# A conv and attention block whose order of work is planned ahead: product and hidden buffers handed out by the plan, other planning numbers, another table of places

## Chip, cores and metric

The kernel runs on one core of one Trainium2 chip. The metric is the device time of one execution in microseconds. The kernel before took 4097.11 us, the median of 3 runs (4096.09 to 4097.49).

## What is computed

The reference is one transformer block on x of 16 images, 128 channels, 96 x 96 pixels, in float32:

```python
xn1 = layernorm(x)                      # over the 128 channels of a pixel
q, k, v = xn1 @ wq.T, xn1 @ wk.T, xn1 @ wv.T
a = softmax(l2norm(q) @ l2norm(k).T * 0.25)   # 8 heads, 16 x 16 over channels
x = x + (a @ v) @ wp.T
h1 = conv1x1(layernorm(x), w_in)        # 128 -> 512 channels
h3 = gelu(depthwise_conv3x3(h1, w_dw))
out = x + conv1x1(h3, w_out)            # 512 -> 128
```

## The kernel before, in words

Channels lie on the 128 partitions. An image is 8 bands of 12 rows; band g runs over all 16 images (128 bands). The 512 hidden channels are 4 chunks of 128. A **conv job** (g, n) is the depthwise convolution of chunk n of band g, 12 x 96 = 1152 elements a partition. There are 470 jobs with accumulating DMAs and one last job without. In some bands chunk 3 is done by matmuls instead (`by_matmuls`, L1037, gelu L1047).

One conv job goes through all engines. TensorE makes h1 (L928) into one of four PSUM banks; ScalarE copies it to the job's `h1` tile (L933, and two halo rows by L924). Of the nine taps, ScalarE makes three as products (L944, tiles `pr`), GpSimd adds the first product and the centre tap into `merged` (L947), and VectorE does the remaining five: the **first tap** (L956, `acc<-h,ratio,merged`, the only tap with two inputs in SBUF), three taps on the PSUM accumulator (L960), and the **last tap**, which writes the tile `h3` (L956, `h<-h,ratio,acc`). The other two products come in by DMA: the **first add** (L969, `pr<-pr`) adds the third product to the second, and the **second add** (L972, `h<-pr`) adds that sum to `h3`. Both are issued by GpSimd. ScalarE then does the gelu (L976) in place in `h3`, four matmuls a third of a band (L1065) give the output, VectorE adds it to x (L1072) and SyncE stores it (L1076).

Beside the jobs runs the normalization of the next image (names with `a`) and of the next band (`b`), 288 groups of 512 pixels each: transposes (L654, L658), a copy by ScalarE to a tile `zT` (L690), statistics on VectorE (L665), variance, power and scaling on GpSimd (L670, L674, L696), and transposes back on TensorE (L741), which ScalarE places in `xn` (L745, L747). The attention matmuls with the image's mixing matrix (L606) give x after attention, by ScalarE (L615), to which an accumulating DMA adds x (L618, GpSimd). SyncE loads x (L586).

The order of all this is written by a planner at build time (class `Plan`, L76 on). Each piece of work is recorded by `op` with its engine, an estimated duration, what it reads and writes, and a place: the job's number plus an offset out of the table `AT` (a few kinds have a `RANK` too). `order` then plays the pieces through: whenever an engine is idle it takes the ready piece with the lowest place. A piece is ready when those it needs have ended by plan, `SLACK` included. For an accumulating DMA the end is one serial line: `max(issue + WAIT, line) + T_ADD`, plus a margin. The planner also hands out buffers (`free`, `slot`): a piece that needs a new buffer waits until one is free by plan, and gets the one that was freed longest ago. The pieces are emitted in the order of their planned starts; on the chip each engine works through its own instructions in that order and waits for semaphores.

In the kernel before, the tiles `pr` (7 buffers) and `h3` (8) came from rotating pools (`prp`, `h3p`): the planner's numbers for them paced the plan, but which buffer a tile really got was decided by the pool.

`two` marks pieces that share a lock in the planner: first taps on VectorE, and the merge L947 and the scaling L696 on GpSimd. A marked GpSimd piece waits for a running first tap, and a first tap waits for a running marked GpSimd piece.

Of the kernel before, what the change touches and what calls it, by code (L numbers as in the profile page):

```python
# [18 lines left out]
BR = 12  # L19
# [17 lines left out]
QT = 4  # L37
# [9 lines left out]
ZT_BUFS = 7  # L47
IN_TURN = ("zT", "tr", "h3", "pr", "xb", "x1")
AT = dict(
    load_w=8.85, weights=-1115.55, zeros=-3007.1, load_a=9.15, forth_a=-13.45, stats_a=342.05, variance_a=451.45,  # L50
    power_a=3765.3, pool_product=152.05, merge=371.35, scaled_a=3441.05, gram=419.9, back_a=415.35, place_a=450.55,
    attention=4.2, mix=1645.7, residual=204, mixed=450.15, add_x=3459.55, forth_b=-8.15, stats_b=-221.5,
    variance_b=332.25, power_b=311.5, shift_b=20.9, scaled_b=245.4, back_b=-36.7, place_b=740.05, halo=1030.45,
    hidden=418.25, kept=-261.05, products=719.4, add_last=374.1, tap=4.75, add_first=-2841.6, gelu=934.15,
    conv=420.9, conv_gelu=4.6, out=422.4, add=-1132.95, store=144.25, mix_0=441.5, residual_0=6.4, mixed_0=991.85,
    add_x_0=3457.3, gram_0=-32.2, forth_a_0=1643.1, forth_b_0=-7.6, stats_a_0=-369.9, stats_b_0=511.45,
    scaled_a_0=-2763, copied_a=-1171.4, copied_b=-1171.6, copied_a_0=4, copied_b_0=906.8, scaled_b_0=451.9,
    back_a_0=-31.55, back_b_0=260.7, place_a_0=995.05, place_b_0=577.35, shift_b_0=22.8, late=-369.55,
)
RANK = dict(tap=-1415.25, products=337.1, forth_a=-1411.95, forth_b=-1558.5, conv_gelu=-1485.55, mix=-1412.45)  # L60
STEP = dict(scaled=0.3, hidden=0.1, products=0.5, tap=0.166, conv=1.6, conv_tap=0.03, out=0.8, out_part=0.05)
SLACK = 300
NORM1_END = 6.0
EARLY = 5
WAIT = dict(POOL=350, SP=1300, ACT=1300)
T_START = 2300
T_VARIANCE = 420
T_POWER = 350 + 165 * QT * QB
T_SMALL = 220
T_MERGE = 2400  # L70
T_POOL_PRODUCT = 1190
T_SCALED = 225
T_ADD, T_MOVE = 3060, 1640


class Place(float):  # L76
# [8 lines left out]
class Plan:  # L85
# [44 lines left out]
    def order(self):  # L130
        ops, free = self.ops, self.free
        left = [len(o[4]) for o in ops]
        followers = [[] for _ in ops]
        for k, o in enumerate(ops):
            for d in o[4]:
                followers[d].append(k)
        held = [[] for _ in ops]
        pending = {}
        for t, ks in self.users.items():
            pending[t] = len(ks)  # L140
            for k in ks:
                held[k].append(t)
        queues, idle, waiting = {}, {}, {}
        queue_of = {p: [] for p in free}
        for k, o in enumerate(ops):
            queues.setdefault(o[0], [])
            idle[o[0]] = True
            for t in o[5]:
                queue_of[t[0]].append((getattr(o[2], "turn", o[2]), k))
        turn = {p: sorted(q)[::-1] for p, q in queue_of.items()}  # L150
        events, starts, count = [], [None] * len(ops), 0

        def push(time, kind, what):
            nonlocal count
            count += 1
            heapq.heappush(events, (time, count, kind, what))

        def room(k):
            need = {}
            for t in ops[k][5]:  # L160
                need[t[0]] = need.get(t[0], 0) + 1
                if t[0] in IN_TURN and turn[t[0]][-1][1] != k:
                    return t[0]
            for p, n in need.items():
                if len(free[p]) < n:
                    return p
            return None

        def dispatch(engine, time):
            queue = queues[engine]  # L170
            while queue:
                item = heapq.heappop(queue)
                k = item[1]
                lacks = room(k)
                if lacks is None:
                    break
                waiting.setdefault(lacks, []).append(k)
            else:
                return
            o = ops[k]  # L180
            starts[k] = time
            idle[engine] = False
            for t in o[5]:
                self.slot[t] = free[t[0]].pop(0)
                if t[0] in IN_TURN:
                    turn[t[0]].pop()
                    wake(t[0], time)
            ns, result, own = o[1], o[6], o[7]
            if o[8]:
                self.dma = max(time + ns + WAIT[engine], self.dma) + o[8]  # L190
                result = own = self.dma + result - time
            elif engine == "POOL" and o[9]:
                rest = max(0, self.two - time)
                ns, result, own = rest + ns, rest + result, rest + own
                self.held = time + ns
            if o[9] and engine == "DVE":
                rest = max(0, self.held - time)
                ns, result, own = rest + ns, rest + result, rest + own
                self.two = time + ns
                self.lost += rest  # L200
            push(time + own, "own", k)
            push(time + ns, "idle", k)
            push(time + result, "done", k)

        def wake(pool, time):
            for k in waiting.pop(pool, ()):
                heapq.heappush(queues[ops[k][0]], (ops[k][2], k))
                push(time, "look", ops[k][0])

        for k, o in enumerate(ops):  # L210
            if not left[k]:
                heapq.heappush(queues[o[0]], (o[2], k))
        for e in queues:
            push(0.0, "look", e)
        while events:
            time, _, kind, what = heapq.heappop(events)
            if kind != "look":
                for f in followers[what] if kind != "idle" else ():
                    if (ops[f][0] == ops[what][0]) == (kind == "own"):
                        left[f] -= 1  # L220
                        if not left[f]:
                            heapq.heappush(queues[ops[f][0]], (ops[f][2], f))
                            push(time, "look", ops[f][0])
            if kind == "done":
                for t in held[what]:
                    pending[t] -= 1
                    if not pending[t]:
                        free[t[0]].append(self.slot[t])
                        wake(t[0], time)
            if kind in ("done", "own"):  # L230
                continue
            if kind == "idle":
                what = ops[what][0]
                idle[what] = True
            if idle[what]:
                dispatch(what, time)
        assert None not in starts, "the buffers do not suffice"
        self.end = max(starts)
        return [ops[k][3] for k in sorted(range(len(ops)), key=lambda k: (starts[k], k))]
# [3 lines left out]
def tile_restormer_block(  # L243
# [101 lines left out]
    att = ctx.enter_context(tc.tile_pool(name="att", bufs=1))  # L345
    keep = ctx.enter_context(tc.tile_pool(name="keep", bufs=2))
    h1p = ctx.enter_context(tc.tile_pool(name="h1p", bufs=1))
    prp = ctx.enter_context(tc.tile_pool(name="prp", bufs=PR_BUFS))
    h3p = ctx.enter_context(tc.tile_pool(name="h3p", bufs=H3_BUFS))

# [1 line left out]


    merged = h1p.tile([P, BR, W], F32, name="merged")
    zT_bufs = [h1p.tile([P, QT, P + 1], F32, name=f"zT_{k}") for k in range(ZT_BUFS)]

    def window(t, r, n, dx=0):
# [18 lines left out]

    def z_unit(i, u):
        return ("z", ring_of(i, u * UR) // UR)  # L380

    def rows(t):
        return t.rearrange("p (r w) -> p r w", w=W)
# [42 lines left out]
        op("POOL", ns, p, f, r, w, ns + 80 + SLACK, ns + 80, two=port)  # L426

    def add(p, f, r, w):
        op("POOL", 930, p, f, r, w, 1400 + SLACK, dma=T_ADD)

    def move(p, f, r, w, ns, first=0):
        op("SP", 60 + first, p, f, r, w, 900 + SLACK, dma=ns)
# [16 lines left out]
    def weights(p):  # L449
# [2 lines left out]
        v, names = staged, iter(range(99))  # L452

        def loads():
            a, b = (h3p.tile([P, BR * W], F32, tag="h3", name=f"weights_{k}") for k in range(2))
            v["win"] = a[:, :HID].rearrange("p (n c) -> p n c", c=P)
            v["wout"], v["wp"] = a[:, HID : 2 * HID], a[:, 2 * HID : 2 * HID + P]
            v["wqk"], v["wqkT"] = b[:, : 2 * P], b[:, 2 * P : 4 * P]
# [131 lines left out]
    def norm(i, second, place_of):  # L590
# [41 lines left out]
        def pixels(s, m):  # L632
# [43 lines left out]
            def zT(q):  # L676
# [3 lines left out]
                    zTs[q] = zT_bufs[plan.slot["zT", (name, q)]]  # L680
                    return zTs[q]
                two = [k for k in (q - q % 2, q - q % 2 + 1)]
                t = h3p.tile([P, BR * W], F32, tag="h3", name=f"zT_{two[0]}")
                for k in two:
                    zTs[k] = t[:, k % 2 * QT * (P + 1) : (k % 2 + 1) * QT * (P + 1)].rearrange("p (t c) -> p t c", c=P + 1)
                    nc.gpsimd.memset(zTs[k][:, :, P:], 1.0)
# [93 lines left out]
    def attention(s, i):  # L780
# [27 lines left out]
            nc.scalar.copy(sb([P, P + 1], "gs"), grams[i][:, : P + 1])  # L808
            v["gsb"], v["s"] = v["gs"][:, :P], v["gs"][:, P:]

        @step("PE", 760)
        def _():

            nc.tensor.matmul(ps([P, 2 * P], "ps_u"), lhsT=v["gsb"], rhs=wqkT, start=True, stop=True)
# [18 lines left out]
        def _():  # L833
            nc.vector.tensor_mul(v["prod"], v["ps_u"], wqkT)

        @step("PE", 1100, wide)
        def _():
            pn, pc = ps([P, 2], "ps_n"), ps([P, 2], "ps_c")
            for z in range(2):
# [6 lines left out]
            nc.tensor.matmul(kq, lhsT=v["sk"], rhs=cqk[:, :P], start=False, stop=False)  # L846
            nc.tensor.matmul(kq, lhsT=cqk[:, P:], rhs=v["sqn"], start=False, stop=True)

        @step("DVE", 320)
        def _():  # L850

            n2 = sb([P, 2], "n2")
# [21 lines left out]

            nc.scalar.activation(sb([P, P], "e"), v["ps_qk"], AF.Exp, scale=v["rq"])

        @step("DVE", 700)
        def _():
            em = sb([P, P], "em")
            nc.vector.tensor_mul(em, v["e"], blocks)  # L880
# [22 lines left out]

    def h3_of(g, n):
        if (g, n) not in h3s:
            h3s[g, n] = h3p.tile([P, BR, W], F32, tag="h3", name=f"h3_{g}_{n}")
        return h3s[g, n]

    def conv_job(j, g, n):
# [27 lines left out]
            return window(h1_, dy, BR, dx)  # L937

        def product(t):
            to = d["pr", t] = prp.tile([P, BR, W], F32, tag="pr", name=f"pr_{g}_{n}_{t}")  # L940
            if t == by_pool:
                nc.gpsimd.tensor_scalar(to, shifted(t), ratio[:, n, t : t + 1], 1.0, ALU.mult, ALU.mult)
            else:
# [206 lines left out]
```

## Time and profile before

| what | value |
|---|---|
| runs, median of 3 | 4097.11 us (4096.09 to 4097.49) |
| the profiled execution, its own time | 4102.16 us |
| span of its instructions | 4100.5 us |
| instructions | 52124 |
| mean granted TensorE clock | 0.994 |
| busy share TensorE, VectorE, ScalarE, GpSimd | 96%, 95%, 91%, 85% |

The page gives each engine's busy time and, for groups of equal instructions, the idle time of the engine just before them with what ended it. The view of waits sums such idle time by who waited for whom. The timeline gives single instructions with their start and duration. On GpSimd and VectorE a recorded duration can hold a wait inside it, which shows only as a duration above that of the shortest of its kind.

### The profile page before, as it was taken

The numbers are of one execution on the slowest core, as the hardware profiler recorded it, in microseconds if no ns is written. First come the engines' busy times: TensorE is split into PE (matmuls) and PEld (weight loads), VectorE is DVE, ScalarE is ACT, GpSimd is POOL, SyncE is SP. The second block draws the span as 40 slices with busy tenths as digits, with TensorE's granted clock in tenths as the row PEclk, the third lists the DMA queues.
The fourth block names the chain that finished last, engine by engine and source line by source line (L and its number), as shares of the span: only waits on it lengthen the run. The fifth ranks groups of instructions, "written<-read, shape, count | busy, mean of one in ns | idle before, by whom it ended". The sixth has DMA issues, their size and how long they took to land.

```text
span 4100.5 us, 52124 instructions
## 1 busy us (share of the span) xinstructions
PE 3932.9 (96%) x17409; PEld 2600.1 (63%) x17409; DVE 3893.5 (95%) x4170; ACT 3716.6 (91%) x5675; POOL 3492.2 (85%) x3320
## 2 busy tenths in 40 slices
PE   8999999999999999999999999999999999999999
PEld 7666566666666666666666666666666666666555
DVE  6999999999999999999999999999999999999997
ACT  4999899999999999989999989999999999899895
POOL 6979799897988979979798898989989899798774
PEclk9999999999999999999999999999999999999999
DMA  3899989899999989989999989999999999898996
GB/s 92 177 191 198 193 188 195 187 199 193 202 192 204 193 185 204 205 191 203 195 207 184 205 188 196 211 190 212 192 194 199 194 199 189 195 192 178 190 186 141
DMA packets 192845, 782.19 MB, mean 191 GB/s; under 512 B 22336, under 2 KB 23744, under 8 KB 192576
## 3 DMA queue, kind: packets, MB, share of 16 engines
q0 software_dynamic: 153072, 627.05, 80.3%
q1 hardware_dynamic: 38256, 151.73, 10.2%
q8 instruction: 136, 2.23, 0.2%
q14 instruction: 133, 1.09, 0.1%
q10 hardware_dynamic: 1248, 0.09, 0.0%
HBM read 148.85 MB, written 75.50 MB: 55 GB/s over the span
## 4 chain that ended last, share of the span: by engine, by line
PE 30%; DVE 25%; POOL 16%; DMA 12%; ACT 10%; issue 7%; POOLq 0%; DVEq 0%; ACTq 0%
DVE acc L960 12%; PE h L1065 7%; PE h L1037 7%; PE h L928 6%; DMA pr<-pr 5%; DMA h<-pr 5%; DVE acc L956 5%; POOL merged L947 4%; DVE h L956 4%; ACT pr L944 4%; POOL zT L696 3%; PE h L606 2%; PE h L741 2%; PE g L703 2%; PE h L654 2%
## 5 line engine op out<-in xcount | busy, mean ns | idle before, releaser
L960 DVE SCALAR_TENSOR_TENSOR acc<-h,ratio,acc 128x1140 f32<-128x1140 f32 (+2 forms) x1416 | 1948.6, 1376 | 18.5
L944 ACT ACTIVATE pr<-h,ratio 128x1152 f32<-128x1152 f32 x1410 | 1784.1, 1293 | 72.3 <-DMA h<-pr 33.4
L947 POOL TENSOR_TENSOR merged<-pr,h 128x1152 f32<-128x1152 f32 x470 | 1298.6, 2763 | 82.5 <-ACT pr L944 44.0
L928 PE MATMUL h<-xn,winT 128*128 128x384 f32 (+1 forms) x2826 | 1102.6, 495 | 27.9 <-ACT zT L690 10.7
L1065 PE MATMUL h<-h,woutT 128*128 128x384 f32 x3072 | 1108.1, 488 | 15.2 <-ACT h L976 7.4
L1037 PE MATMUL h<-xn,comp 128*128 128x380 f32 (+2 forms) x2214 | 805.4, 482 | 2.7 <-ACT h L1047 0.9
L1065 PEld LDWEIGHTS h<-h,woutT 128*128 128x128 f32 x3072 | 562.3, 190 | 367.5 <-issue 12.1
L956 DVE SCALAR_TENSOR_TENSOR acc<-h,ratio,merged 128x1152 f32<-128x1152 f32 x470 | 736.9, 1568 | 37.6 <-POOL merged L947 21.8
L933 ACT COPY h<-h 128x384 f32<-128x384 f32 (+2 forms) x1413 | 680.6, 514 | 77.6 <-PE h L928 72.4
L972 POOL DMA_DIRECT2D h<-pr x470 | 529.0, 1126 | 236.2 <-DVE h L956 56.8
L928 PEld LDWEIGHTS h<-xn,winT 128*128 128x128 f32 x2826 | 499.5, 190 | 326.3 <-ACT zT L690 23.5
L956 DVE SCALAR_TENSOR_TENSOR h<-h,ratio,acc 128x1152 f32<-128x1152 f32 x471 | 661.6, 1405 | 8.4 <-PE h L1065 1.7
L969 POOL DMA_DIRECT2D pr<-pr x470 | 548.0, 1174 | 133.2 <-ACT pr L944 98.0
L976 ACT ACTIVATE h<-h 128x1152 f32<-128x1152 f32 (+1 forms) x473 | 563.1, 1191 | 60.9 <-DMA h<-pr 54.5
L1037 PEld LDWEIGHTS h<-xn,comp 128*128 128x128 f32 x2214 | 399.4, 190 | 235.9 <-issue 15.9
L696 POOL TENSOR_TENSOR zT<-zT,rstd_a 128x512 f32<-128x512 f32 (+1 forms) x288 | 438.7, 1563 | 4.0
L674 POOL TENSOR_TENSOR rstd_a<-ve_a,mhalf 128x4 f32<-128x4 f32 x288 | 437.9, 1624 | 3.7
L741 PEld LDWEIGHTS h<-ident,zT 128*128 128x128 f32 x2304 | 283.4, 141 | 230.0 <-issue 74.5
L741 PE MATMUL h<-ident,zT 128*128 128x128 f32 x2304 | 372.0, 277 | 47.7 <-POOL zT L696 34.8
L696 POOL TENSOR_TENSOR zT<-zT,rstd_b 128x512 f32<-128x512 f32 (+1 forms) x288 | 372.3, 1294 | 5.2
L690 ACT COPY zT<-h 128x512 f32<-128x512 f32 x553 | 322.1, 614 | 53.7 <-PE h L654 34.6
L674 POOL TENSOR_TENSOR rstd_b<-ve_b,mhalf 128x4 f32<-128x4 f32 x288 | 361.5, 1255 | 9.9
(170 smaller groups left out, 4329.6 us busy)
## 6 DMA issues: line engine op xcount, KB each, us to landing
pr<-pr POOLq DMA_DIRECT2D x470, 576.0 KB, 7.4
h<-pr POOLq DMA_DIRECT2D x470, 576.0 KB, 7.4
x<-in_x_dram SPq DMA_DIRECT2D x128, 576.0 KB, 6.8
out_dram<-x SPq DMA_DIRECT2D x127, 576.0 KB, 5.8
x<-in_x_dram POOLq DMA_DIRECT2D x123, 576.0 KB, 7.6
out_dram<-x SPq DMA_DIRECT2D x3, 192.0 KB, 1.9
weights<-in_L_conv_w_in_dram SPq DMA_DIRECT2D x1, 256.0 KB, 3.2
weights<-in_L_conv_w_out_dram SPq DMA_DIRECT2D x1, 256.0 KB, 3.4
```

The source lines that it names most:

```text
L674: nc.gpsimd.tensor_tensor(rstd, d["ve"], mhalf, ALU.pow)
L696: engine.tensor_tensor(z, z, rstd.unsqueeze(2).to_broadcast([P, len(ks), P]), ALU.mult)
L741: nc.tensor.transpose(d["pB"][:, j * P : (j + 1) * P], zTs[q][:, k, :P], ident)
L928: nc.tensor.matmul(rows(ph), lhsT=winT[:, n, :], rhs=window(xn, r0 + r, e - r, 1), start=True, stop=True)
L933: nc.scalar.copy(window(h1_, r, e - r, 1), rows(d.pop(("ph", r))))
L944: nc.scalar.activation(to, shifted(t), AF.Copy, scale=ratio[:, n, t : t + 1])
L947: nc.gpsimd.tensor_tensor(merged, d["pr", dma_taps[0]], shifted(UNIT), ALU.add)
L956: nc.vector.scalar_tensor_tensor(to, shifted(t), ratio[:, n, t : t + 1], also, ALU.mult, ALU.add)
L960: nc.vector.scalar_tensor_tensor(to, shifted(t)[:, lo:hi, cut], ratio[:, n, t : t + 1], to, ALU.mult, ALU.add)
L976: nc.scalar.activation(h3, h3, AF.Gelu)
L1037: nc.tensor.matmul(d["pc"][:, lo:hi, cut], lhsT=comp[:, t, :], rhs=window(xn, r0 + dy, UR, dx)[:, lo:hi, cut], start=(t == order[0]), stop ...
L1065: nc.tensor.matmul(rows(d["po"]), lhsT=woutT[:, n, :], rhs=h3s[g, n][:, s * UR : (s + 1) * UR, :], start=(k == 0), stop=(k == NCH - 1),)
```

## The change

The amount of work is the same: every engine has the same instructions, in another order. Four things differ.

1. `pr` and `h3` are 7 and 8 single tiles, and a piece uses the one that the planner handed out.
2. In `order`, every GpSimd piece that is no DMA issue now waits for a running first tap, not only the merge and the scaling; only these two still hold up a first tap.
3. Planned durations and margins: `SLACK` 300 to 150; GpSimd's `WAIT` 350 to 1090, `T_ADD` 3060 to 2950, `T_MOVE` 1640 to 1400, the margin behind an accumulating DMA's landing from 1400 + 300 to 500 + 150, its issue 930 to 890, four steps of the attention longer (all in the planner's ns).
4. Another table `AT`, `RANK`; their values alone say nothing, the rows below show what they do.

```diff
-SLACK = 300
+SLACK = 150
-WAIT = dict(POOL=350, SP=1300, ACT=1300)
+WAIT = dict(POOL=1090, SP=1300, ACT=1300)
-T_POWER = 350 + 165 * QT * QB
-T_SMALL = 220
+T_POWER = 360 + 165 * QT * QB
+T_SMALL = 190
-T_ADD, T_MOVE = 3060, 1640
+T_ADD, T_MOVE, T_LAND = 2950, 1400, 500
...
-            elif engine == "POOL" and o[9]:
+            elif engine == "POOL":
                 rest = max(0, self.two - time)
                 ns, result, own = rest + ns, rest + result, rest + own
-                self.held = time + ns
+                if o[9]:
+                    self.held = time + ns
...
-    prp = ctx.enter_context(tc.tile_pool(name="prp", bufs=PR_BUFS))
-    h3p = ctx.enter_context(tc.tile_pool(name="h3p", bufs=H3_BUFS))
+    pr_bufs = [h1p.tile([P, BR, W], F32, name=f"pr_{k}") for k in range(PR_BUFS)]
+    h3_bufs = [h1p.tile([P, BR, W], F32, name=f"h3_{k}") for k in range(H3_BUFS)]
...
-        op("POOL", 930, p, f, r, w, 1400 + SLACK, dma=T_ADD)
+        op("POOL", 890, p, f, r, w, T_LAND + SLACK, dma=T_ADD)
...
-            h3s[g, n] = h3p.tile([P, BR, W], F32, tag="h3", name=f"h3_{g}_{n}")
+            h3s[g, n] = h3_bufs[plan.slot["h3", (g, n)]]
...
-            to = d["pr", t] = prp.tile([P, BR, W], F32, tag="pr", name=f"pr_{g}_{n}_{t}")
+            to = d["pr", t] = pr_bufs[plan.slot["pr", (jn, t)]]
```

Two places show what the order becomes. First GpSimd, in the middle of the program, before: names are `pr_band_chunk_tap` and `h3_band_chunk`.

```order
L947 TENSOR_TENSOR merged_147<-pr_54_2_3_12835,h1_2_145 128x1152
L674 TENSOR_TENSOR rstd_b7_1_12889<-ve_b7_1_12867,mhalf_93 128x4
L969 DMA pr_54_2_5_12853<-pr_54_2_1_12861 128x1152
L696 TENSOR_TENSOR zT_0_148<-zT_0_148,rstd_b7_1_12889 128x4x128
L670 TENSOR_SCALAR ve_a8_2_12910<-st_a8_2_12873 128x4
L618 DMA x2_7_1_12833<-in_x_dram 128x1152
L972 DMA h3_54_1_12903<-pr_54_1_5_12794 128x1152
```

The third product of job (55, 1), `pr_55_1_0`, got the memory of `pr_54_1_5`, which the last of these rows still reads. The planner had handed out the buffer of `pr_54_2_1`, which the third row, four rows earlier, reads. After the change the numbers in `pr_k` are the buffers themselves; the same engine, merge of (55, 0) to first add of (55, 1) (line numbers are 4 higher: L951 is the merge, L973 and L976 the first and second add, L948 a product, L980 the gelu):

```order
L951 TENSOR_TENSOR merged_141<-pr_6_148,h1_0_137 128x1152
L973 DMA pr_0_142<-pr_2_144 128x1152
L976 DMA h3_4_153<-pr_1_143 128x1152
L674 TENSOR_SCALAR ve_b7_2_12155<-st_b7_2_12140 128x4
L678 TENSOR_TENSOR rstd_b7_2_12161<-ve_b7_2_12155,mhalf_93 128x4
L951 TENSOR_TENSOR merged_141<-pr_3_145,h1_1_138 128x1152
L700 TENSOR_TENSOR zT_0_157<-zT_0_157,rstd_b7_2_12161 128x4x128
L674 TENSOR_SCALAR ve_b7_3_12188<-st_b7_3_12158 128x4
L973 DMA pr_5_147<-pr_6_148 128x1152
```

The third product of (55, 1), now `pr_6` in the last row, takes the buffer that the merge in the first row read last: it waits for that merge, and for no DMA.

Second ScalarE, two bands on, before: the three products of job (57, 1), and the gelu of (56, 2).

```order
L944 ACTIVATE pr_57_1_3_13455<-h1_1_144,ratio_106 128x1152
L944 ACTIVATE pr_57_1_5_13464<-h1_1_144,ratio_106 128x1152
L944 ACTIVATE pr_57_1_1_13469<-h1_1_144,ratio_106 128x1152
L933 COPY h1_2_145<-h_3_76 128x4x96
L933 COPY h1_2_145<-h_1_74 128x4x96
L933 COPY h1_2_145<-h_0_73 128x4x96
L1047 ACTIVATE h3_57_3_13490<-h_2_75 128x384
L745 ACTIVATE xn_124<-h_3_76,b2_101 128x4x96
L976 ACTIVATE h3_56_2_13385<-h3_56_2_13385 128x1152
```

The same piece of ScalarE's program after the change, where `h3_3` is the tile of (56, 2) and `pr_4`, `pr_2`, `pr_3` are the products of (57, 1):

```order
L948 ACTIVATE pr_4_146<-h1_1_138,ratio_106 128x1152
L948 ACTIVATE pr_2_144<-h1_1_138,ratio_106 128x1152
L1051 ACTIVATE h3_2_151<-h_3_76 128x384
L980 ACTIVATE h3_3_152<-h3_3_152 128x1152
L937 COPY h1_2_139<-h_2_75 128x4x96
L749 ACTIVATE xn_124<-h_1_74,b2_101 128x4x96
L948 ACTIVATE pr_3_145<-h1_1_138,ratio_106 128x1152
```

The gelu of (56, 2) stood behind all three products and three h1 copies of later jobs; it now stands behind two products and no h1 copy of job (57, 2).

More of the change, by code (lines that the diff above doesn't have):

```diff
@@ L49 @@
 AT = dict(
[L50 to L58, printed above, removed]
+    load_w=-15.9, weights=1106.95, zeros=-4389.1, load_a=-21.95, forth_a=-14.05, stats_a=1086.6,
@@ new lines @@
+    variance_a=-3642.25, power_a=-2095.25, pool_product=152.05, merge=-3089.75, scaled_a=-3192.7, gram=420.15,
+    back_a=-250, place_a=-142.6, attention=-21.5, mix=810.75, residual=204, mixed=-263.1, add_x=-3629.7,
+    forth_b=-10.3, stats_b=962.7, variance_b=-3011.35, power_b=-3726.4, shift_b=20.9, scaled_b=-4386.5,
+    back_b=285.25, place_b=-290.45, halo=-471.5, hidden=418.3, kept=-390.75, products=-596.2, add_last=-2869,
+    tap=3.65, add_first=-4251.35, gelu=-9.7, conv=421.7, conv_gelu=4.3, out=422.65, add=865.75, store=-21.95,
@@ L59 @@
+    mix_0=421.5, residual_0=864.15, mixed_0=-612, add_x_0=-4213.25, gram_0=419.75, forth_a_0=-276.85,
+    forth_b_0=-13.8, stats_a_0=1145.4, stats_b_0=866.4, scaled_a_0=-4479.8, copied_a=-299.2, copied_b=-393.1,
+    copied_a_0=-390.45, copied_b_0=-1293.75, scaled_b_0=-3010.5, back_a_0=420.4, back_b_0=262, place_a_0=-286.8,
+    place_b_0=11.4, shift_b_0=22.8, late=384.05,
 )
-RANK = dict(tap=-1415.25, products=337.1, forth_a=-1411.95, forth_b=-1558.5, conv_gelu=-1485.55, mix=-1412.45)
+RANK = dict(tap=-69.4, products=649.2, forth_a=-922.65, forth_b=-118.15, conv_gelu=-62.7, mix=-456.4)
@@ L61 @@
 STEP = dict(scaled=0.3, hidden=0.1, products=0.5, tap=0.166, conv=1.6, conv_tap=0.03, out=0.8, out_part=0.05)
-SLACK = 300
+SLACK = 150
 NORM1_END = 6.0
 EARLY = 5
-WAIT = dict(POOL=350, SP=1300, ACT=1300)
+WAIT = dict(POOL=1090, SP=1300, ACT=1300)
 T_START = 2300
-T_VARIANCE = 420
-T_POWER = 350 + 165 * QT * QB
-T_SMALL = 220
+T_POWER = 360 + 165 * QT * QB
+T_SMALL = 190
 T_MERGE = 2400
@@ L380, in z_unit, with flat @@
         return ("z", ring_of(i, u * UR) // UR)
+    def flat(t):
+        return t.rearrange("p r w -> p (r w)")
     def rows(t):
@@ L454, in loads @@
         def loads():
-            a, b = (h3p.tile([P, BR * W], F32, tag="h3", name=f"weights_{k}") for k in range(2))
+            a, b = (flat(h3_bufs[plan.slot["h3", ("weights", k)]]) for k in range(2))
             v["win"] = a[:, :HID].rearrange("p (n c) -> p n c", c=P)
@@ L682, in zT @@
                 two = [k for k in (q - q % 2, q - q % 2 + 1)]
-                t = h3p.tile([P, BR * W], F32, tag="h3", name=f"zT_{two[0]}")
+                t = flat(h3_bufs[plan.slot["h3", ("zT", q // 2)]])
                 for k in two:
@@ L809, in _ @@
             v["gsb"], v["s"] = v["gs"][:, :P], v["gs"][:, P:]
-        @step("PE", 760)
+        @step("PE", 1060)
         def _():
@@ L834, in _ @@
             nc.vector.tensor_mul(v["prod"], v["ps_u"], wqkT)
-        @step("PE", 1100, wide)
+        @step("PE", 1850, wide)
         def _():
@@ L847, in _ @@
             nc.tensor.matmul(kq, lhsT=cqk[:, P:], rhs=v["sqn"], start=False, stop=True)
-        @step("DVE", 320)
+        @step("DVE", 670)
         def _():
@@ L875, in _ @@
             nc.scalar.activation(sb([P, P], "e"), v["ps_qk"], AF.Exp, scale=v["rq"])
-        @step("DVE", 700)
+        @step("DVE", 1060)
         def _():
```

## The prediction, as it was put on record

> **What bounds the kernel now.** I read the page's first lines, then the busy time by stage, then who VectorE waits for.
>
> ```profile
> span 4100.5 us, 52124 instructions
> PE 3932.9 (96%) x17409; PEld 2600.1 (63%) x17409; DVE 3893.5 (95%) x4170; ACT 3716.6 (91%) x5675; POOL 3492.2 (85%) x3320
> PE 30%; DVE 25%; POOL 16%; DMA 12%; ACT 10%; issue 7%; POOLq 0%; DVEq 0%; ACTq 0%
> ```
>
> The chain changes engine all the time, so no engine alone is the bound, and the whole idle time of VectorE is 4100.5 - 3893.5 = 207.0 us. By stage (busy us of PE, PEld, DVE, ACT, POOL):
>
> ```profile
> 0.00:100.00 100.00, 86.07 (x577) 74.67 (x578) 60.59 (x164) 45.41 (x92) 66.78 (x139) 0.95 0.30 92
> 100.00:3600.00 3500.00, 3369.32 (x14998) 2227.31 (x14997) 3372.61 (x3566) 3251.02 (x4968) 3067.51 (x2869) 1.00 0.93 196
> 4000.00:4100.50 100.50, 96.87 (x327) 58.51 (x325) 79.53 (x71) 57.44 (x81) 39.66 (x34) 1.00 0.64 139
> ```
>
> VectorE is idle 39 us in the first 100 and 21 in the last 100.5; both ends are the same chains in either order, and I take them as unchanged. In 3500 us between it is idle 127 us, 3.6%. That, and waits hidden in its durations, is all that another order can win.
>
> ```profile
> DVE x L1072 <- PE h L1065: 47.8, 46, 5.4
> DVE st_b L665 <- ACT zT L690: 31.8, 28, 3.9
> DVE acc L956 <- POOL merged L947: 21.8, 23, 2.3
> DVE st_a L665 <- ACT zT L690: 16.6, 12, 5.8
> ACT h L933 <- PE h L928: 72.4, 135, 2.1
> ```
>
> VectorE waits for every other engine, for none of them long. So each term below is first an idle time of another engine, and only a part reaches VectorE. For ScalarE I set that part from these rows: it is idle 4100.5 - 3716.6 = 383.9 us, and VectorE's waits with ScalarE at their root are 31.8 + 16.6 + 21.8 = 70.2 us (merges wait for products): 0.18. For TensorE, idle 167.6 us with 47.8 us of VectorE behind it: 0.29.
>
> **How distances are counted.** Trace and program list each engine's instructions in one order, so each row of the trace can be set beside its place in the program; numbers got so are called joined. The distance of a producer from its consumer is the VectorE work written between them, each instruction at its row's mean. Where I say "by distance", I took the wait found at each distance in the trace of before and gave it to the distances of the new order.
>
> **Product buffers.** The products that waited for an accumulating DMA to let go of their buffer, with the first, the longest and the last such wait:
>
> ```profile
>   DMA h<-pr: 33.4, 22
>   DMA pr<-pr: 32.6, 35
> 196.70 1.26 ACT L944 ACTIVATE pr<-h,ratio 128x1152 f32<-128x1152 f32 x1 [0.31 <-DMA pr<-pr]
> 1825.87 1.25 ACT L944 ACTIVATE pr<-h,ratio 128x1152 f32<-128x1152 f32 x1 [4.26 <-DMA h<-pr]
> 3950.82 2.40 ACT L944 ACTIVATE pr<-h,ratio 128x1152 f32<-128x1152 f32 x2 [0.43 <-DMA pr<-pr]
> ```
>
> Joined, 739 of 1410 products lay in a buffer whose last user was not the one that the planner had counted on, and they hold 55 of the 57 waits and 64.0 of the 66.0 us; the 4.26 us are the first GpSimd piece shown above. With the planner's own buffers these go: ScalarE -64, on VectorE 64 x 0.18 = **-11.5**. Bounds: nothing (the copies' wait for TensorE at L933, 72.4 us above, takes their place) to all 64. What is late next on ScalarE is the gelu.
>
> **Gelus move towards their DMA.**
>
> ```profile
> L976 ACT ACTIVATE h<-h 128x1152 f32<-128x1152 f32 (+1 forms) x473 | 563.1, 1191 | 60.9 <-DMA h<-pr 54.5 <-DVE h L956 5.7
> 122.40 1.17 ACT L976 ACTIVATE h<-h 128x1152 f32<-128x1152 f32 x1 [0.58 <-DMA h<-pr]
> 4058.49 1.17 ACT L976 ACTIVATE h<-h 128x1152 f32<-128x1152 f32 x1 [1.43 <-DMA h<-pr]
> h<-pr POOLq DMA_DIRECT2D x470, 576.0 KB, 7.4
> ```
>
> Between a second add and its gelu the old order has 10.08 us of VectorE work in the mean, the new one 8.77; below the 7.4 us that a landing takes lie 45 gelus, then 103. By distance the wait grows from 54 to 75 us: ScalarE +21, VectorE **+3.8**. Upper bound: if each gelu really came 1.3 us nearer to its landing, the 470 joined landings give 212 us of waiting, +158. Behind a waiting gelu stand the copies L933 and L690 that TensorE and VectorE's statistics need. The Trainium skill, "DMA: Bandwidth & Descriptors", Anatomy of one DMA, gives 2.0 us plus bytes / 436e3 for such a transfer, an estimate of 3.4 us for 576 KB. By that no gelu of either order would wait, and the sum would be 14 us lower; the 7.4 us row, queueing included, and the 54.5 us of waits say otherwise, and I stay with them.
>
> **Products move ahead of the merges.**
>
> ```profile
> L947 POOL TENSOR_TENSOR merged<-pr,h 128x1152 f32<-128x1152 f32 x470 | 1298.6, 2763 | 82.5 <-ACT pr L944 44.0 <-DVE acc L956 29.9 <-ACT zT L690 3.0
> L969 POOL DMA_DIRECT2D pr<-pr x470 | 548.0, 1174 | 133.2 <-ACT pr L944 98.0 <-ACT h L924 15.8 <-DVE h L956 4.5
> ```
>
> A first product stands 4.75 us of VectorE work ahead of its merge before, 6.87 after. By distance the merges' wait falls from 41 to 18 us and the first adds' from 97 to 75. GpSimd is busy 85%, so its own idle time counts little. What counts are the first taps behind the merges: their distance hardly moves, and by distance their 21 us become 18: **-3**, with 0 and -21.8 as bounds. In the same way the statistics gain **-3** (their copies stand 0.5 us further ahead) and the adds L1072 lose **+1**.
>
> **First taps behind a scaling.**
>
> ```profile
> L956 DVE SCALAR_TENSOR_TENSOR acc<-h,ratio,merged 128x1152 f32<-128x1152 f32 x470 | 736.9, 1568 | 37.6 <-POOL merged L947 21.8 <-DVE h L956 0.5
> L956 DVE SCALAR_TENSOR_TENSOR h<-h,ratio,acc 128x1152 f32<-128x1152 f32 x471 | 661.6, 1405 | 8.4 <-PE h L1065 1.7
> 104.87 1.28 POOL L696 TENSOR_TENSOR zT<-zT,rstd_a 128x512 f32<-128x512 f32 x1
> 105.18 2.21 DVE L956 SCALAR_TENSOR_TENSOR acc<-h,ratio,merged 128x1152 f32<-128x1152 f32 x1
> 3900.95 1.04 POOL L696 TENSOR_TENSOR zT<-zT,rstd_b 128x512 f32<-128x512 f32 x1
> 3901.11 2.10 DVE L956 SCALAR_TENSOR_TENSOR acc<-h,ratio,merged 128x1152 f32<-128x1152 f32 x1
> ```
>
> A first tap takes 163 ns more than a last tap of the same size, 470 x 0.163 = 77 us in all: a wait that counts as busy. The pairs show it: the tap that starts while a scaling L696 runs ends about 1.2 us after the scaling's end. Joined, 88 taps are longer by over 0.15 us, 80 of them start beside a scaling, and those hold 59.6 us. In the old order 218 first taps have a scaling written within 3 us ahead of them, in the new one 171, 22% fewer: 0.22 x 59.6 = **-13**, on VectorE itself and in full. Bounds: -77 (all gone) and +13 (the planned gaps don't survive on the chip and as many more are hit).
>
> **Transposes behind a scaling.**
>
> ```profile
> L741 PEld LDWEIGHTS h<-ident,zT 128*128 128x128 f32 x2304 | 283.4, 141 | 230.0 <-issue 74.5 <-POOL zT L696 67.5 <-ACT x L615 7.5
> L741 PE MATMUL h<-ident,zT 128*128 128x128 f32 x2304 | 372.0, 277 | 47.7 <-POOL zT L696 34.8 <-ACT x L615 3.2 <-ACT xn L747 3.1
> ```
>
> The scaling's median distance to its transposes falls from 8.2 to 5.1 us, since the new plan lets GpSimd be late. By distance TensorE's wait rises from 32 to 48 us: 16 x 0.29 = **+4.6**. Bounds 0 and, if the two rows' 102 us double, +30. TensorE's next matmuls, h1 and outputs, queue behind.
>
> **Sum.** -11.5 + 3.8 - 3 - 3 + 1 - 13 + 4.6 = -21 us on the profiled execution's own 4102.2 us: 4081. That execution is 5.1 us above the median of the runs, 4097.1, so I forecast **4076 us**.
>
> **Rivals.**
>
> *The gelu takes the place of the buffer (slower).* The new plan keeps 650 ns behind a planned landing where it kept 1700, and sees all DMAs as one line. The queue rows speak for trouble:
>
> ```profile
> q0 software_dynamic: 153072, 627.05, 80.3%
> q1 hardware_dynamic: 38256, 151.73, 10.2%
> ```
>
> The engines are busy 90% of the span, and loads and stores have 10.2% of it, 418 us over 263 transfers, 1.6 us each, about what the margin was. If an add shares the engines with them instead of standing in line, landings slip past the margin. The Trainium skill says so in "DMA: Bandwidth & Descriptors", Issuing engines are not separate DMA queues: transfers of all issuers interleave on the same engines. With the full +158 us ScalarE is 94 us worse off; if half reaches the end, +47, and with the other terms (-13) 4097 + 34 = 4131 us. It decides from a shift of about 0.9 us (joined waits 147 us, +93 against -64, half of 29 against the other 13). Against it: landings were slower than planned before too, and at 10 us distance still few waited.
>
> *ScalarE's time passes in full (much faster).* If ScalarE's waits sit on the chain (DMA has 12% of it, nine of the 57 joined waits exceed 2 us), -64 + 21 count whole instead of by 0.18: 4102 - 56 - 5 = 4041 us.
>
> *Hidden (no change).* The removed waits only let ScalarE arrive earlier at its next wait for TensorE, and the distance to scalings is lost in the drift of the engines: 4097 us, give or take 6.
>
> *It does not do what it says.* The buffers freed by plan are still read on the chip, since the margin is smaller, and product waits stay at 66 us: 4087 us, which lies in the forecast's own range.
>
> **How the numbers follow.** Forecast, 4060 to 4088: 0.43. In full, around 4041: 0.19. Hidden: 0.13. Gelu, around 4131: 0.19; transposes at their upper bound with the buffers' gain hidden, 4097 + 30 - 13 = 4114: 0.06. 0.2% (8 us) is about what a measurement of this kernel can tell from no change, so faster 0.62, same 0.13, slower 0.25. The range takes in the full case and the gelu's: 4035 to 4132.
>
> **What would show it.** Right: products' waits for DMAs below 10 us in all; gelus' wait 60 to 100 us; first taps' mean near 1540 ns; merges' wait for products near 20 us; VectorE idle near 200 us. Wrong: gelus waiting over 140 us, or a first tap's mean at or above 1568 ns.

## The result, and the profile after

The changed kernel takes 4105.82 us (median of 20 runs, 4092.32 to 4117.26), the kernel before in the same series 4097.45 us (20 runs, 4088.48 to 4102.77). The ratio is 1.0019, with a 95% interval of 1.0010 to 1.0029. So it is slower, by 0.2%, where 0.5% faster was forecast. The runs also scatter more: 25 us from the fastest to the slowest, 14 us before.

The profiled execution of the changed kernel (4102.59 us, 3 us under its median) and that of before (4102.16 us) are equally long. They show what changed inside. The page's first lines and its groups of products, merges, first taps, gelus and first adds (lines 4 higher than before):

```profile
span 4100.9 us, 52028 instructions
PE 3936.4 (96%) x17409; PEld 2593.9 (63%) x17409; DVE 3904.0 (95%) x4170; ACT 3718.0 (91%) x5675; POOL 3456.0 (84%) x3320
...
L948 ACT ACTIVATE pr<-h,ratio 128x1152 f32<-128x1152 f32 x1410 | 1782.5, 1289 | 45.2 <-DMA pr<-pr 27.3
L951 POOL TENSOR_TENSOR merged<-pr,h 128x1152 f32<-128x1152 f32 x470 | 1249.5, 2659 | 72.8 <-DVE acc L960 44.8
...
L960 DVE SCALAR_TENSOR_TENSOR acc<-h,ratio,merged 128x1152 f32<-128x1152 f32 x470 | 753.2, 1602 | 26.8 <-POOL merged L951 11.6
...
L980 ACT ACTIVATE h<-h 128x1152 f32<-128x1152 f32 (+1 forms) x473 | 561.4, 1187 | 101.7 <-DMA h<-pr 94.6
L973 POOL DMA_DIRECT2D pr<-pr x470 | 492.9, 1055 | 136.9 <-ACT pr L948 100.5
```

And who waited for whom:

```profile
ACT h L980 <- DMA h<-pr: 94.6, 96, 4.5
PEld h L745 <- POOL zT L700: 67.1, 95, 4.3
DVE x L1076 <- PE h L1069: 51.8, 52, 5.5
ACT pr L948 <- DMA pr<-pr: 27.3, 26, 4.4
DVE st_b L669 <- ACT zT L694: 21.1, 29, 1.8
POOL merged L951 <- ACT pr L948: 20.6, 18, 3.3
PE h L658 <- DMA x<-in_x_dram: 15.2, 18, 2.3
ACT pr L948 <- POOL merged L951: 13.2, 13, 3.3
DVE acc L960 <- POOL merged L951: 11.6, 10, 2.7
DVE st_a L669 <- ACT h L694: 8.9, 4, 5.7
DVE st_a L669 <- ACT zT L694: 1.9, 5, 0.7
```

Some copies of the first 50 us go into `h3` buffers and now have their name (`h`) instead of `zT`, so the statistics' wait for copies, two rows before, is three rows here: 21.1 + 8.9 + 1.9 = 31.9 us.

Products' waits for DMAs fell from 66.0 to 27.3 us, and gelus' waits rose from 54.5 to 94.6 (56 times before, 96 now): on ScalarE one took the place of the other (120.5 us before, 121.9 now). VectorE is idle 196.9 us, 10 less than before, but its busy time is 3904.0, 10.5 more: the first taps have a mean of 1602 ns against 1568, 470 x 0.034 = 16 us, and the rest of its work 6 us less.

### The profile page after: what moved, and what is told of

Same layout as the page of the kernel before. It is cut to its first block, busy times and chain, and to the rows that moved or that the text cites. A ratio compares the mean times of both kernels' runs of the same rounds, so it can differ in the third digit from the quotient of the medians.

```text
span 4100.9 us, 52028 instructions
## 1 busy us (share of the span) xinstructions
PE 3936.4 (96%) x17409; PEld 2593.9 (63%) x17409; DVE 3904.0 (95%) x4170; ACT 3718.0 (91%) x5675; POOL 3456.0 (84%) x3320
## 4 chain that ended last, share of the span: by engine, by line
PE 31%; DVE 20%; DMA 11%; ACT 11%; POOL 9%; issue 5%; POOLq 0%; DVEq 0%; SPq 0%; ACTq 0%
PE h L1069 9%; DVE acc L964 9%; PE h L932 7%; DMA h<-pr 6%; PE h L1041 5%; ACT pr L948 4%; DVE acc L960 4%; DVE h L960 3%; POOL merged L951 3%; DMA x<-in_x_dram 3%; PE h L658 2%; PE h L610 2%; PE h L745 2%; DMA pr<-pr 2%; POOL zT L700 2%
## 5 line engine op out<-in xcount | busy, mean ns | idle before, releaser
L948 ACT ACTIVATE pr<-h,ratio 128x1152 f32<-128x1152 f32 x1410 | 1782.5, 1289 | 45.2 <-DMA pr<-pr 27.3
L951 POOL TENSOR_TENSOR merged<-pr,h 128x1152 f32<-128x1152 f32 x470 | 1249.5, 2659 | 72.8 <-DVE acc L960 44.8
L1069 PE MATMUL h<-h,woutT 128*128 128x384 f32 x3072 | 1122.3, 489 | 11.7 <-DVE x L1076 7.1
L932 PE MATMUL h<-xn,winT 128*128 128x384 f32 (+2 forms) x2826 | 1086.4, 495 | 24.2 <-DVE x L1076 9.0
L960 DVE SCALAR_TENSOR_TENSOR acc<-h,ratio,merged 128x1152 f32<-128x1152 f32 x470 | 753.2, 1602 | 26.8 <-POOL merged L951 11.6
L976 POOL DMA_DIRECT2D h<-pr x470 | 496.0, 1056 | 253.3 <-PE h L1069 39.3
L980 ACT ACTIVATE h<-h 128x1152 f32<-128x1152 f32 (+1 forms) x473 | 561.4, 1187 | 101.7 <-DMA h<-pr 94.6
L973 POOL DMA_DIRECT2D pr<-pr x470 | 492.9, 1055 | 136.9 <-ACT pr L948 100.5
L678 POOL TENSOR_TENSOR rstd_a<-ve_a,mhalf 128x4 f32<-128x4 f32 x288 | 416.4, 1521 | 1.0
L745 PE MATMUL h<-ident,zT 128*128 128x128 f32 x2232 | 357.5, 276 | 49.8 <-POOL zT L700 31.8
L700 POOL TENSOR_TENSOR zT<-zT,rstd_a 128x512 f32<-128x512 f32 x270 | 384.9, 1451 | 1.9
L700 POOL TENSOR_TENSOR zT<-zT,rstd_b 128x512 f32<-128x512 f32 (+1 forms) x288 | 357.7, 1243 | 5.2
```

The lines of the kernel that those rows point to most:

```text
L678: nc.gpsimd.tensor_tensor(rstd, d["ve"], mhalf, ALU.pow)
L700: engine.tensor_tensor(z, z, rstd.unsqueeze(2).to_broadcast([P, len(ks), P]), ALU.mult)
L745: nc.tensor.transpose(d["pB"][:, j * P : (j + 1) * P], zTs[q][:, k, :P], ident)
L932: nc.tensor.matmul(rows(ph), lhsT=winT[:, n, :], rhs=window(xn, r0 + r, e - r, 1), start=True, stop=True)
L948: nc.scalar.activation(to, shifted(t), AF.Copy, scale=ratio[:, n, t : t + 1])
L951: nc.gpsimd.tensor_tensor(merged, d["pr", dma_taps[0]], shifted(UNIT), ALU.add)
```

## The experiments

Two theories stood at the start. **G**: own buffers gain as forecast, and gelus planned nearer to their DMA give it back. **L**: the buffers are hidden, and the longer first taps decide. All kernels compute the whole block. Times are compared as ratios to the kernel before, run beside them on the same chip.

### The parts apart

Own tiles in the order of before, instruction for instruction (only part 1 of the change), and the reverse, the changed order with rotating pools:

```diff
 # e1_own_tiles: before, with
-    prp = ctx.enter_context(tc.tile_pool(name="prp", bufs=PR_BUFS))
+    pr_bufs = [h1p.tile([P, BR, W], F32, name=f"pr_{k}") for k in range(PR_BUFS)]
 # (h3 likewise)
 # e2_pools: after, with
-    pr_bufs = [h1p.tile([P, BR, W], F32, name=f"pr_{k}") for k in range(PR_BUFS)]
+    prp = ctx.enter_context(tc.tile_pool(name="prp", bufs=PR_BUFS))
 # (h3 likewise)
```

> The order of before, instruction for instruction; only product and hidden tiles are the single buffers that the planner hands out. Theory G (own buffers gain, and the shorter distance of the gelus to their DMA gives it back in the full change): the products' wait for DMAs falls from 66 to under 10 us, gelu waits stay near 54 us, and the time falls by 11 us (0.18 of 64) or more, to 4086 or below. Theory L (the first taps behind a scaling decide, the buffers are hidden): products' wait falls the same way, the first taps' mean stays near 1568 ns, and the time stays within 4 us of 4097.

> The order of the changed kernel, but product and hidden tiles out of rotating pools as before. Theory G: products' waits for DMAs come back to some 60 us, and the time rises by about 11 us over the changed kernel, to 4117. Theory L: no difference from the changed kernel over 4 us, 4102 to 4110, with the first taps' mean still near 1600 ns.

Own tiles alone: 4073.04 us, ratio 0.9943 (0.9932 to 0.9955). Pools in the changed order: 4150.12 us, 1.0130 (1.0117 to 1.0144). ScalarE's waits in the first:

```profile
ACT h L979 <- DMA h<-pr: 65.5, 62, 3.2
ACT pr L947 <- POOL merged L950: 19.1, 21, 4.1
ACT pr L947 <- DMA pr<-pr: 6.3, 6, 1.9
```

and VectorE's busy time and waits there:

```profile
PE 3916.6 (96%) x17409; PEld 2591.3 (64%) x17409; DVE 3886.2 (95%) x4170; ACT 3715.3 (91%) x5675; POOL 3489.5 (86%) x3320
```

```profile
DVE x L1075 <- PE h L1068: 45.6, 48, 5.4
DVE acc L959 <- POOL merged L950: 20.9, 23, 2.3
DVE st_b L668 <- ACT zT L693: 14.2, 20, 2.5
DVE st_a L668 <- ACT h L693: 10.4, 4, 5.4
DVE st_a L668 <- ACT zT L693: 7.0, 9, 1.8
```

ScalarE's waits in the second:

```profile
ACT h L980 <- DMA h<-pr: 63.5, 64, 4.5
ACT pr L948 <- DMA pr<-pr: 60.5, 55, 4.4
ACT pr L948 <- DMA h<-pr: 51.1, 28, 4.0
```

Same order, other buffers, and the products' wait for DMAs goes from 66.0 to 6.3 us in one, from 27.3 to 111.6 in the other. The buffers are worth 0.57% or 23 us in the old order and 1.1%, 45 us, in the new one. They are not hidden, which is against L; G, too, had put the second loss at only 11 us. Then the rest of the change costs what they gain and more: from 4073 to 4106.

The rest apart, each with own tiles: the new planning numbers and rule with the old table (e3), and the new table with the old numbers and rule (e4).

```diff
 # e3_model_alone: after, with before's AT and RANK
 # e4_table_alone: e1_own_tiles, with after's AT and RANK
```

> Own buffers, the new waiting rule, durations and margins, but before's table of places and ranks. Theory G: the shorter margin alone brings the gelus nearer, so gelu waits of 80 us or more, and no gain from the buffers: 4095 to 4110. Theory L: the new rule makes GpSimd's plan truer, first taps' mean at or below 1568 ns and a time at or below 4097. A table that was fitted to other numbers may also cost 10 us or more by itself, which neither theory tells.

> Own buffers and the new table, with before's rule, durations and margins. Theory G: gelus keep their distance, gelu waits near 54 us, products' waits under 15 us, time at or below 4090. Theory L: scalings are placed by the new table, first taps' mean near 1600 ns, time 4100 to 4110.

e3: 4108.54 us, 1.0035 (1.0022 to 1.0048). e4: 4125.73 us, 1.0069 (1.0057 to 1.0081). Each alone is worse than both together (1.0019), as if the table were fitted to its numbers. e3 came as G had it: gelu waits of 114.7 us, and a loss although its first taps are short (1548 ns), where L expected 4097 us or less. e4 came as neither had it (gelu waits 65.1 us, first taps 1579 ns), so these two don't decide.

### Which number

From e1 on (own tiles, old table) one edit each, with a control that only reshuffles the order:

```diff
 # c1_jitter
-T_MERGE = 2400
+T_MERGE = 2405
 # e5_slack
-SLACK = 300
+SLACK = 150
 # e6_dma
-WAIT = dict(POOL=350, SP=1300, ACT=1300)
+WAIT = dict(POOL=1090, SP=1300, ACT=1300)
-T_ADD, T_MOVE = 3060, 1640
+T_ADD, T_MOVE, T_LAND = 2950, 1400, 500
-        op("POOL", 930, p, f, r, w, 1400 + SLACK, dma=T_ADD)
+        op("POOL", 890, p, f, r, w, T_LAND + SLACK, dma=T_ADD)
 # e7_rule
-            elif engine == "POOL" and o[9]:
+            elif engine == "POOL":
 # (held only if o[9], as in the change)
 # e10_land_only
-        op("POOL", 930, p, f, r, w, 1400 + SLACK, dma=T_ADD)
+        op("POOL", 930, p, f, r, w, 500 + SLACK, dma=T_ADD)
```

> The kernel with own tiles and before's table and numbers (4073 us), in which the planner's estimate of a merge is 2405 instead of 2400 ns. That says nothing new about the chip, but reorders a quarter of VectorE's rows and a third of ScalarE's. Theory F (a table of places fits only the numbers it was made with, so any replanning loses): 4095 to 4115 us, as much as the meaningful changes. Theory M (the shorter margins cost): within 8 us of 4073, gelu waits near 65 us.

> The same kernel with SLACK 150 instead of 300, nothing else. Theory M: consumers are planned 150 ns nearer to everything, gelu waits 75 us or more, product waits for DMAs 15 us or more, 4085 to 4100 us. Theory F: 4095 to 4115, no more than the jitter costs.

> The same kernel with the new numbers for accumulating DMAs and moves alone (WAIT 1090, T_ADD 2950, T_MOVE 1400, 500 instead of 1400 ns behind a landing, issue 890). Theory M: gelu waits 85 us or more, products' waits for DMAs 15 us or more, 4090 to 4105 us. Theory F: as the jitter, within 8 us of it.

> The same kernel with the new rule alone: every GpSimd piece but a DMA issue waits in the plan for a running first tap. Theory M: no harm, within 8 us of 4073, first taps' mean at or below 1557 ns, since the plan is truer. Theory F: as the jitter, 4095 to 4115.

> The kernel with own tiles and before's table, rule and numbers (4073 us), but 500 instead of 1400 ns behind a planned landing. Theory M: most of what all new DMA numbers cost (68 us): gelu waits 100 us or more, 4110 to 4145. Theory P: within 10 us of 4073; the loss with all DMA numbers would then come from the order that the other three give.

| kernel | us | ratio to before | interval | products' / gelus' wait for DMAs, us |
|---|---|---|---|---|
| e1, own tiles | 4073.04 | 0.9943 | 0.9932 to 0.9955 | 6.3 / 65.5 |
| c1, merge + 5 ns | 4076.11 | 0.9940 | 0.9925 to 0.9955 | 7.9 / 59.4 |
| e5, SLACK 150 | 4085.15 | 0.9964 | 0.9951 to 0.9976 | 7.4 / 39.6 |
| e7, rule | 4126.49 | 1.0056 | 1.0036 to 1.0077 | 5.7 / 66.5 |
| e6, DMA numbers | 4145.50 | 1.0108 | 1.0091 to 1.0125 | 15.8 / 111.7 |
| e10, 500 behind a landing | 4156.87 | 1.0147 | 1.0129 to 1.0165 | 14.0 / 103.3 |

The control changes nothing, though it reorders the program as much as the others do (place by place, 61% of VectorE's instructions differ in kind from e1's, with e5 61%, with e10 60%). So the table stands a meaningless shift, and F, the theory that any replanning loses, falls. Halving `SLACK` comes out 9 us slower, but the intervals of e1 and e5 overlap, so that is unclear; its gelu waits fell to 39.6 us where M expected 75 or more, so the sum of gelu waits alone doesn't tell the time. The margin behind a landing, 1400 to 500, alone costs 84 us, more than the new DMA numbers together (68 us, a longer `WAIT` among them); both losses are larger than M expected. The rule costs 46 us with the table that wasn't made for it, where M expected no harm.

The same from the other side, in the changed kernel with its own table:

```diff
 # c2_after_jitter: T_MERGE 2405
 # e8_after_land
-T_ADD, T_MOVE, T_LAND = 2950, 1400, 500
+T_ADD, T_MOVE, T_LAND = 2950, 1400, 1400
 # e9_after_norule
-            elif engine == "POOL":
+            elif engine == "POOL" and o[9]:
```

> The changed kernel with the planner's merge at 2405 instead of 2400 ns: a control for how far a meaningless replanning moves it. Both theories: within 10 us of 4106.

> The changed kernel with the margin behind a planned landing of an accumulating DMA put back from 500 to 1400 ns, all else as changed. Theory M (that margin costs): gelu waits fall from 95 us to 50 or less, products' waits for DMAs from 27 to under 10, time 4075 to 4095. Theory P (the new waiting rule, and the places that the table has for it, cost): gelu waits fall too, but the time stays within 10 us of 4106.

> The changed kernel without the new rule: in the plan only the merge and the scaling wait for a running first tap. Theory M: within 10 us of 4106, gelu waits near 95 us. Theory P: 4080 to 4095. A table that was fitted to the rule could make it slower instead, above 4116.

c2: 4117.11 us, 1.0051 (1.0034 to 1.0069), just past the 10 us that were expected. e9: 4110.03 us, 1.0034 (1.0020 to 1.0047). e8: 4071.00 us, 0.9935 (0.9919 to 0.9951). A meaningless shift moves the changed kernel by up to 0.3%, so differences below some 13 us mean little there. Taking the rule away is within that. Putting the margin back wins 0.84%, 34 us. Its page and its waits:

```profile
PE 3924.2 (96%) x17409; PEld 2602.7 (64%) x17409; DVE 3894.6 (96%) x4170; ACT 3714.3 (91%) x5675; POOL 3438.5 (84%) x3320
L960 DVE SCALAR_TENSOR_TENSOR acc<-h,ratio,merged 128x1152 f32<-128x1152 f32 x470 | 748.0, 1591 | 36.0 <-POOL merged L951 20.7
```

```profile
ACT h L980 <- DMA h<-pr: 69.4, 60, 5.3
ACT pr L948 <- DMA pr<-pr: 10.0, 15, 1.4
DVE st_b L669 <- ACT zT L694: 12.8, 14, 2.1
DVE x L1076 <- PE h L1069: 44.1, 40, 4.6
```

The first taps are nearly as long as in the changed kernel (1591 against 1602 ns), and yet 34 us are back: L falls. What went is waiting for landings: 42 us on ScalarE (27.3 + 94.6 to 10.0 + 69.4), more than half of the wait of the transposes' matmuls for x (15.2 to 5.9 us), and, behind it, VectorE's waits for ScalarE's copies (31.9 to 22.2) and TensorE's outputs (51.8 to 44.1). VectorE is idle 21 us less in all and busy 9 us less. The gelu waits were expected to fall further, to 50 us.

### Which landing, and how much margin

A landing's margin delays, in the plan, the gelu and the buffer of the second product (second add), the second add and the buffer of the third product (first add), and the transposes of x (L618, now L622).

```diff
 # e12_second_add: 1400 behind the second add, 500 behind the others
 # e13_first_add: 500 behind the second add, 1400 behind the others
 # e14_after_2000: T_LAND = 2000;   e15_after_2600: T_LAND = 2600
 # e16_second_2000: 2000 behind the second add, 500 behind the others
 # e11_land_more: e1_own_tiles, with 2000 + SLACK instead of 1400 + SLACK
```

> The changed kernel, with 1400 ns behind the landing of the second add alone (gelu, and the buffer of the second product); the first add and the x transfer keep 500. Theory G (the gelu is what the margin protects): 4071 to 4085 us, gelu waits 70 us or less. Theory B (buffers and the second add behind the first add): within 10 us of 4106.

> The reverse: 1400 ns behind the first add and the x transfer, 500 behind the second add. Theory G: within 10 us of 4106, gelu waits 90 us or more. Theory B: 4071 to 4085 us, products' waits for DMAs under 10 us.

> The changed kernel with 2000 ns behind every landing. If landings are still later than planned, gelu waits fall from 69 to 40 us and the time to 4055 to 4068; if 1400 was enough, buffers are held longer for nothing and the time is 4071 to 4090.

> Own tiles with before's table and numbers, and 2000 instead of 1400 ns behind a landing. As for the changed kernel: 4055 to 4068 if landings are still later than planned (gelu waits 65 to 40 us), 4073 to 4095 if not.

> The changed kernel with 2600 ns behind every landing. If 2000 had used up what the landings need (18 us of gelu waits are left), buffers are held longer for nothing and the time is 4029 to 4060; if landings are still late, 4005 to 4025.

> The changed kernel with 2000 ns behind the second add alone, 500 behind the others. Theory G (the gelu): gelu waits under 30 us and 4029 to 4055 us. Theory B (first add, buffers and x transfer carry as much): 4065 to 4085, with gelu waits as low.

| kernel | us | ratio to before | interval | products' / gelus' wait for DMAs, us | gelus with under 7.4 us of VectorE work between their add and them |
|---|---|---|---|---|---|
| after, 500 | 4105.82 | 1.0019 | 1.0010 to 1.0029 | 27.3 / 94.6 | 103 |
| e13, 500 for the second add | 4111.34 | 1.0025 | 1.0015 to 1.0035 | 12.4 / 109.1 | 116 |
| e12, 1400 for the second add | 4082.80 | 0.9946 | 0.9932 to 0.9961 | 21.2 / 49.8 | 50 |
| e8, 1400 | 4071.00 | 0.9935 | 0.9919 to 0.9951 | 10.0 / 69.4 | 35 |
| e16, 2000 for the second add | 4094.08 | 0.9992 | 0.9982 to 1.0001 | 19.6 / 21.9 | 13 |
| **e14, 2000** | **4028.96** | **0.9813** | **0.9799 to 0.9828** | 7.0 / 18.3 | 18 |
| e15, 2600 | 4062.51 | 0.9912 | 0.9895 to 0.9928 | 1.0 / 11.7 | 6 |
| e11, 2000, old table and numbers | 4094.18 | 0.9975 | 0.9964 to 0.9987 | 2.0 / 31.4 | 26 |

The last column, counted as in the prediction, goes with the gelus' waits only roughly (e8 has fewer near gelus than e12 and longer waits).

Between 500 and 1400 the second add carries the effect (30 of the 34 us are back in e12, none in e13, though in e12 the transposes' matmuls still wait 23.6 us for x). In the changed kernel no product waits for a second add's landing (its 27.3 us name the first add, `pr<-pr`), so it is the gelu that the margin protected. But e16 sets a bound to that. It has few gelu waits left and is no better than the kernel before, outside what both theories expected, while the same margin behind all landings gives 4029 us. So the waits of gelus alone don't make the time; what else the margin behind the other landings moves counts too. In e16 TensorE's transposes still waited for the x transfer (18.0 us on their matmuls), and in e14 hardly (0.6), but I didn't separate that from the first add. The page and waits of e14, and the first taps of e15:

```profile
span 4026.0 us, 52020 instructions
PE 3905.8 (97%) x17409; PEld 2589.8 (64%) x17409; DVE 3874.7 (96%) x4170; ACT 3709.1 (92%) x5675; POOL 3464.0 (86%) x3320
L960 DVE SCALAR_TENSOR_TENSOR acc<-h,ratio,merged 128x1152 f32<-128x1152 f32 x470 | 728.2, 1549 | 34.5 <-POOL merged L951 18.2
```

```profile
L960 DVE SCALAR_TENSOR_TENSOR acc<-h,ratio,merged 128x1152 f32<-128x1152 f32 x470 | 753.6, 1603 | 36.2 <-POOL merged L951 20.0 <-DVE h L960 0.5
```

```profile
DVE x L1076 <- PE h L1069: 35.2, 34, 5.5
ACT h L980 <- DMA h<-pr: 18.3, 26, 2.0
DVE st_b L669 <- ACT zT L694: 9.5, 11, 1.8
ACT pr L948 <- DMA pr<-pr: 7.0, 10, 1.0
```

At 1.9% under the kernel before e14 is the fastest of all, faster than either of its expectations. 2600, just above its expectation, loses 41 us again by ratio, with almost no wait for a DMA left, and with the old table 2000 is worse than 1400. Part of this is not the margin's aim. Against e8, VectorE is idle 25 us less in e14 (176.1 to 151.3), but also busy 20 us less, all of it in first taps (748.0 to 728.2), and in e15 the first taps take 25 us more again (753.6). The margin doesn't plan for the first taps; how many are hit by a scaling differs from order to order. So some 20 us of e14's gain and 25 us of e15's loss look like luck of one order, and how much of the rest is luck stays open; the controls moved by 0 and 0.3%.

## Why the prediction was wrong

The forecast said 4076 us; 4105.82 came, inside the range (4035 to 4132), on the other side of no change.

- **Product buffers (-11.5): right in kind, too small.** Alone they gain 23 us. The products' wait for DMAs fell by 60 us, as forecast, and though half of that came back as other waits of ScalarE (for merges 0.3 to 19.1 us, of gelus 54.5 to 65.5), 0.4 of it (23 of 60) reached the end and not 0.18. The factor was an average over all of ScalarE's idle time, and these waits were worth more: the very rows that it was made of fell by 18 us (the statistics' wait for copies from 48.4 to 31.6, the first taps' for merges from 21.8 to 20.9). VectorE's busy time, which it left out, fell by 7 us, and the adds' wait for outputs by 2. In the changed kernel itself the wait fell only to 27.3 us, not below 10, since its margin is smaller: with 1400 ns (e8) it is 10.0. So a part of "it does not do what it says" came too.
- **Gelus move towards their DMA (+3.8): this step failed.** The wait rose by 40 us instead of 21, and the margin that brought the gelus nearer costs 34 us (after against e8; 30 for the second add alone, after against e12), not 4. Its size was wrong twice. Eleven of the 40 us came with own buffers alone, in the old order (54.5 to 65.5 in e1): a ScalarE that no longer waits for buffers waits at its gelus instead, and that isn't in waits taken by distance from before. And the factor 0.18 was far too low again. The rival had the mechanism and its place, but was given only 0.19. Its deciding point was put too high as well: gelu waits of some 147 us, where 95 were enough: between e8 and the changed kernel ScalarE's waits for DMAs differ by 42 us (10.0 + 69.4 against 27.3 + 94.6), and the time by 34.
- **Products move ahead of merges (-3 and less): right in kind.** The merges' wait for products is 20.6 us (18 by distance), VectorE's wait for merges fell from 21.8 to 11.6, and that for copies from 48.4 to 31.9 (21.1 + 8.9 + 1.9). The adds' wait rose by 4 us (+1 forecast). The first adds' wait did not fall (100.5 against 98.0).
- **First taps behind a scaling (-13): wrong in sign.** In the trace 63 long taps start beside a scaling instead of 80, 21% fewer, as the order had it (22%). But each is longer, 0.93 us instead of 0.75, so that together they hold 58.6 us as against 59.6: nothing won. And the long taps into which a scaling comes only after their start went from 7 to 18, from 11 to 28 us. In all +16 us, a first tap's mean of 1602 ns, which the prediction had named as a sign of being wrong. The count could be read from the order, the length of a hit could not. e8 keeps 11 us of this loss and is 27 us faster than before, so it is not what decided.
- **Transposes behind a scaling (+4.6): nothing.** 98.9 us against 102.3.

Along one path, by ratios: own buffers -23 (e1 against before), everything else but the margin -3 (e8 against e1), the margin +34 (after against e8); together +8, as it must be along a path. On another path the shares would be others, since the new numbers and the new table each cost much when put in alone. The margin's sign is sure, with a loss from both sides (84 us from e1, 34 us here); its size goes with the order.

## What to carry to other kernels

Planning a landing too exactly lost time in this kernel: ScalarE works in order, so a gelu whose landing is late holds up all that stands behind it (94.6 us of gelu waits with 500 ns behind a planned landing, 18.3 with 2000). The margin had to cover what landings take under load and not what the fastest take; one order with still more of it (2600 ns) was slower again. When a rotating pool and a planner both decide on buffers, let the planner's choice be the real one (worth 23 us in one order, 45 in the other); the waits that differ are found by setting each wait in the trace beside the buffer's last user. And an engine's average share, here 0.18, is not the price of one kind of its waits: for the products' waits it was 0.4.

## What was not expected of the hardware

An accumulating add of 576 KB landed 6.8 to 7.6 us behind its issue in the median, in all twenty traces, the fastest after 4.8 us, the slowest of a trace after 12.6 to 18.4. A transfer that is alone in the plan lands after 4.9 us without margin (890 + 1090 + 2950 ns), about the fastest that was measured. With margin the fastest order plans 7.1 us (2000 + 150 ns more), the changed kernel 5.6 and the kernel before 6.0. So the constant of a lone transfer was true and still lost time as a plan: the DMA engines are busy 90% of the span, and the medians lie 1.9 to 2.7 us above it.
